# Four convolutions and a perceptron: outputs of two strips in one block

## The chip, the cores and the metric

The kernel runs on one core of a Trainium2 chip. A core has a matrix engine (TensorE, PE in the profile; its weight loads are PEld), a vector engine (VectorE, DVE), an activation engine (ScalarE, ACT), a general engine (GpSimd, POOL) and SyncE (SP), whose instruction queue issues most DMA transfers here. Each engine runs its own queue of instructions, and semaphores order them between engines. Matrix results go to PSUM, eight banks of 128 partitions x 512 float32; VectorE and ScalarE take them from there ("evict" them) to SBUF. The metric is the time of one execution on the device, in microseconds (us).

## The reference

The input is x of shape (4, 16, 512, 512), float32. Four layers follow each other, all with 16 channels in and out:

- layer 0: a depthwise 3x3 convolution with residual, attention in windows of 8x8, and a perceptron with 64 hidden units;
- layer 1: input and weights quantised to 8 bits, a 3x3 convolution, batch normalisation over the whole batch, a clip to 0..6;
- layer 2: two 3x3 convolutions with bias, a ReLU between them, and the input added;
- layer 3: a 3x3 convolution, and then at each pixel a perceptron with 128 hidden units, whose result is added to the layer's input.

Layer 3, which the change touches, is:

```python
y = conv3x3(x, conv_w)                                   # 16 -> 16 channels
h = relu(einsum('bchw,kc->bkhw', y, w1) + b1[None, :, None, None])   # 16 -> 128
upd = einsum('bkhw,ck->bchw', h, w2) + b2[None, :, None, None]       # 128 -> 16
return x + upd
```

## The kernel before

Layer 0 runs first and leaves its result in DRAM. `conv_layers` (L916) does the rest. A first pass over the data gives the statistics of layer 1's convolution; then a second pass, the tail, computes layers 1 to 3 for good. The change is in the tail alone.

**Layout.** The 512 image rows are cut into S = 4 strips of 128 rows, and each strip into M = 64 pairs of rows. One tile holds, for pair mm, all four images and all four strips: 128 partitions are four quarters of 32, and a quarter holds the two rows of the pair with 16 channels each. In the first layers a quarter is a strip and a free index is the image; the last convolution's results have it the other way round after a turn: a quarter is an image and a free index is a strip.

**One step.** The loop `for t in range(-2, M + 7)` (L1169) is a software pipeline. A step has four groups of matrix work, in this order:

1. the convolution of layer 3: it reads `x`, and `done3` (L1099) evicts its four banks to `y`, two by ScalarE and two by VectorE;
2. the second convolution of layer 2: it reads `h`, and `done2` (L1081) evicts to `x` with the residual added, all four by VectorE;
3. the first convolution of layer 2: it reads `z`, and `done1` (L1064) evicts to `h`, two by each engine;
4. the convolution of layer 1 in bfloat16: it reads `q`, and `done0` (L1052) evicts to `z`, all four by ScalarE.

Each convolution works on a different pair, so that a group needs only what earlier groups or steps have left. After group 2, `turned` (L1090) issues 16 DMA copies on SP that bring x into the layout by images (`xi`), for the residual of layer 3.

**A convolution** is 24 turns (`_conv_turn`, L905, matrix instruction in L908). A turn is four matmuls of 32x32 weights on one quarter i of the rows, for the four column quarters, and writes bank i of `conv_banks`. The turns go round the four quarters.

**The perceptron** is cut into units of work. `hidden` (L1112) makes one image's 128 hidden units for one row of one strip: four matmuls of 32x32 weights (L1117) on the quarter of that image into one bank of `hid_banks`, and an eviction with bias and ReLU to a tile `hid`, by ScalarE (L1123) for five of eight, by VectorE (L1125) for three. Eight of them are one strip of one pair. `output` (L1128) makes the results of that strip: eight matmuls with 128 rows and 32 columns (L1131) into `out_bank`, in which the two rows of an image are accumulated, an addition of bias and residual by VectorE (L1137) into `o`, and with the fourth strip the store to DRAM from SP.

**Order.** TensorE, VectorE, ScalarE and SP run in the order in which the program is written (`manual_schedule`); no planner changes it. `group` (L1143) writes the order within a group. It has 32 slots. Slots 4, 7, 10, ... 25 issue one `hidden` each, of the strip that the group was given, and one small piece of other work from the list `between` (a clip of z on VectorE; a scaling on VectorE or a rounding on ScalarE of the next q). The other 24 slots are the convolution's turns. Then come the convolution's evictions, and then `output` for the strip of the group before. So there are four output blocks in a step, one after each group, between the matmuls of one convolution and those of the next.

**Banks.** Of the eight, four are the convolution's, three (`hid_banks`, used in turn) the hidden units', one the outputs'.

Of the kernel before, what the change touches and what calls it, by code (L numbers as in the profile page):

```python
# [11 lines left out]
F32 = mybir.dt.float32  # L12
BF16 = mybir.dt.bfloat16
AF = mybir.ActivationFunctionType
ALU = mybir.AluOpType
# [8 lines left out]
B, C, H, W = 4, 16, 512, 512  # L24
P = 128
# [3 lines left out]
S = 4  # L29
M = H // S // 2  # L30
# [83 lines left out]
def conv_chain(ctx: ExitStack, tc: tile.TileContext, x, xw, mats, vecs, cqs, cws, hots, out):  # L114
# [32 lines left out]
    with tc.If(safe == 0):  # L147
        attention_block(tc, x, x1, m, v, peak)
    conv_layers(tc, x1, out, cw, cq, sw, m, v, peak)


# [728 lines left out]
def _quad(i):  # L880
    return slice(32 * i, 32 * i + 32)
# [18 lines left out]
def _turns():  # L900

    return [(side, dx, i) for side in range(2) for dx in range(3) for i in range(4)]


def _conv_turn(nc, p, weights, src, side, dx, i):  # L905

    for j in range(4):
        nc.tensor.matmul(  # L908
            p[i][_quad(j)], weights[_quad(i), side, dx, :],
            src[side][_quad(i), j, dx : dx + W],  # L910
            start=side == 0 and dx == 0, stop=side == 1 and dx == 2,
        )
# [3 lines left out]
def conv_layers(ctx: ExitStack, tc, x1, out, cw, cq, sw, m, v, peak):  # L916
# [18 lines left out]
    nc = tc.nc  # L935
    ld = ctx.enter_context(tc.tile_pool(name="l3l", bufs=2))
# [1 line left out]
    ps = ctx.enter_context(tc.tile_pool(name="l3p", bufs=1, space=PSUM))  # L938

    banks = [ps.tile([P, W], F32, name=f"tb{i}") for i in range(8)]  # L940
    conv_banks, hid_banks, out_bank = banks[0:4], banks[4:7], banks[7]

    def ring(name, n, dt=F32):
        tiles = []
        for i in range(n):
            t = act.tile([P, 4, WP], dt, name=f"{name}{i}")
            nc.gpsimd.memset(t[:, :, 0 : WP : WP - 1], 0.0)
            tiles.append(t)
        return lambda mm: tiles[mm % n]

    qs = ring("q", 3, BF16)
    zs, hs, xs, xi, ys = ring("z", 3), ring("h", 2), ring("x", 2), ring("xi", 3), ring("y", 2)

    edge_b1 = act.tile([P, 2], F32, name="edge_b1")
    nc.vector.tensor_scalar(edge_b1, v("edge"), v("l2_b1"), None, ALU.mult)
# [13 lines left out]
    def inner(t):  # L969
        return t[:, :, 1 : W + 1]  # L970
# [7 lines left out]
    def load(mm, tag="x"):  # L978
        loaded[mm] = ld.tile([P, S, W], F32, tag=tag, name=f"tx{mm}")
        _load_pairs(nc, loaded[mm], x1, mm)  # L980

    def scaled(mm, at=slice(0, S)):
        t = loaded[mm][:, at]
        nc.vector.tensor_scalar(t, t, ix, ROUND, ALU.mult, ALU.add)

    def rounded(mm, at=slice(0, S)):
        nc.scalar.activation(  # L987
            inner(qs(mm))[:, at], loaded[mm][:, at], AF.Identity, bias=unround
        )
# [9 lines left out]
    for mm in range(M):  # L999
# [5 lines left out]
        p = banks[4 * (mm % 2) : 4 * (mm % 2) + 4]  # L1005
# [19 lines left out]
    def mul(a, b, name):  # L1025
        t = act.tile([P, 1], F32, name=f"mul_{name}")
        nc.vector.tensor_tensor(t, a, b, ALU.mult)
        return t
# [9 lines left out]
    s = mul(sx, sw, "s")  # L1038
# [19 lines left out]
    def clipped(mm, b):  # L1058
        z = inner(zs(mm))
        nc.vector.tensor_scalar(z[:, b], z[:, b], ACT_MAX, None, ALU.min)  # L1060
        if outside(mm) is not None:
            nc.vector.memset(z[_quad(outside(mm)), b], 0.0)  # L1062
# [27 lines left out]
    def turned(mm):  # L1090

        if outside(mm) is None:
            for b in range(B):
                for s in range(S):
                    nc.sync.dma_start(
                        inner(xi(mm))[_quad(b), s, :], inner(xs(mm))[_quad(s), b, :]
                    )
# [10 lines left out]
    w2 = m("w2").rearrange("p (w n) -> p w n", w=2)  # L1108
    count = iter(range(1 << 30))
    waiting, outs = [], {}  # L1110

    def hidden(mm, s, par, b):  # L1112

        k = next(count)
        p = hid_banks[k % 3]
        for c in range(4):
            nc.tensor.matmul(  # L1117
                p[_quad(c)], w1[_quad(b), 1 - par, 32 * c : 32 * c + 32],
                inner(ys(mm + par))[_quad(b), s, :], start=True, stop=True,
            )  # L1120
        hd = ld.tile([P, W], F32, tag="hid", name=f"hid{mm}_{s}_{par}_{b}", bufs=16)
        if k % 8 in (0, 2, 3, 5, 6):
            nc.scalar.activation(hd, p, AF.Relu, bias=v("l3_b1"))  # L1123
        else:
            nc.vector.tensor_scalar(hd, p, v("l3_b1"), 0.0, ALU.add, ALU.max)  # L1125
        return b, par, hd

    def output():  # L1128
        mm, s, hids = waiting.pop(0)
        for b, par, hd in hids:  # L1130
            nc.tensor.matmul(  # L1131
                out_bank[_quad(b), :], w2[:, par], hd, start=par == 0, stop=par == 1
            )
        if s == 0:
            outs["o"] = ld.tile([P, S, W], F32, tag="o", name=f"o{mm}")
        o = outs["o"]
        nc.vector.scalar_tensor_tensor(  # L1137
            o[:, s, :], out_bank, v("l3_b2"), inner(xi(mm))[:, s, :], ALU.add, ALU.add
        )
        if s == S - 1:  # L1140
            nc.sync.dma_start(out[mm], o)

    def group(conv, unit, between):  # L1143


        turns, hids = iter(_turns() if conv else []), []
        for i in range(32):
            q, rest = divmod(i - 4, 3)
            if i >= 4 and rest == 0 and q < 8:
                if unit:  # L1150
                    hids.append(hidden(*unit, q // 4, i % 4))
                if between:
                    between.pop(0)()
            elif conv:
                _conv_turn(nc, conv_banks, conv[0], conv[1], *next(turns))
        for f in between:
            f()
        if conv:
            conv[2]()
        if waiting:  # L1160
            output()
        if unit:
            waiting.append((*unit, hids))

    def conv(layer, rows, lo, done, mm):
        weights = cq if layer is None else cw[:, layer]
        return weights, (rows(lo), rows(lo + 1)), lambda: done(mm)

    for t in range(-2, M + 7):  # L1169
        if t + 3 <= M + 2:  # L1170
            load(t + 3)
        new = [lambda s=s: scaled(t + 2, slice(s, s + 1)) for s in range(S)]
        new += [lambda s=s: rounded(t + 2, slice(s, s + 1)) for s in range(S)]
        clip = [lambda b=b: clipped(t - 1, b) for b in range(B)]
        mm = t - 4
        group(
            conv(2, xs, mm - 1, done3, mm) if 0 <= mm <= M else None,
            (t - 6, 3) if 0 <= t - 6 < M else None,
            clip if -2 <= t - 1 <= M + 1 else [],
        )  # L1180
        mm = t - 3
        group(
            conv(1, hs, mm, done2, mm) if -1 <= mm <= M else None,
            (t - 5, 0) if 0 <= t - 5 < M else None,
            new if t + 2 <= M + 2 else [],
        )
        if -1 <= mm <= M:
            turned(mm)
        mm = t - 1
        group(  # L1190
            conv(0, zs, mm - 1, done1, mm) if -1 <= mm <= M + 1 else None,
            (t - 5, 1) if 0 <= t - 5 < M else None, [],
        )
        mm = t
        group(
            conv(None, qs, mm, done0, mm) if -2 <= mm <= M + 1 else None,
            (t - 5, 2) if 0 <= t - 5 < M else None, [],
        )
    while waiting:
        output()  # L1200


def _strips(a):
# [128 lines left out]
```

## Time and profile before

| what | value |
|---|---|
| median of three runs | 6609.31 us (6609.27 to 6616.03) |
| the profiled execution | 6619.37 us |
| its span | 6617.5 us |
| TensorE busy, share of the span | 6388.5 us, 97% |
| ScalarE busy | 4209.4 us, 64% |
| VectorE busy | 3192.7 us, 48% |
| float32 convolution turns (L908, on z, x and h) | mean 597 to 603 ns a record |
| hidden units, TensorE (L1117) | 16384 records, mean 597 ns |
| hidden units, ScalarE and VectorE | 1280 of 687 ns, 768 of 751 ns |
| outputs, TensorE (L1131) | 4096 records, mean 605 ns |
| outputs, VectorE (L1137) | 256 of 751 ns (median) |

How to read it. The span is the time from the first instruction to the last. A row of the groups gives the line, the engine, the operation, the tile written and the tile read, the shape, the number of records, and after the bar the busy time, the mean of one in ns, and the idle time before it with what ended it. A float32 matmul has two records, one for each of two passes; a bfloat16 one has one. Records on different 32x32 parts of the array overlap, so a busy TensorE is not one at its peak. In the chain of work and in the timeline the first number is the start in us from the start of the span, the second the length of the merged piece, and the number after x is that of the records merged. Brackets give the idle time of the engine just before and what ended it.

### The profile page before, as it was taken

The numbers are of one execution on the slowest core, as the hardware profiler recorded it, in microseconds if no ns is written. First come the engines' busy times: TensorE is split into PE (matmuls) and PEld (weight loads), VectorE is DVE, ScalarE is ACT, GpSimd is POOL, SyncE is SP. The second block draws the span as 40 slices with busy tenths as digits, with TensorE's granted clock in tenths as the row PEclk, the third lists the DMA queues.
The fourth block names the chain that finished last, engine by engine and source line by source line (L and its number), as shares of the span: only waits on it lengthen the run. The fifth ranks groups of instructions, "written<-read, shape, count | busy, mean of one in ns | idle before, by whom it ended". The sixth has DMA issues, their size and how long they took to land. (4 is left out here: it accounts for less than half of the span.)

```text
span 6617.5 us, 317160 instructions
## 1 busy us (share of the span) xinstructions
PE 6388.5 (97%) x146976; PEld 3295.4 (50%) x146976; DVE 3192.7 (48%) x4640; ACT 4209.4 (64%) x5738; POOL 5.9 (0%) x25
## 2 busy tenths in 40 slices
PE   8999999999999999999996689999999999999998
PEld 5555555555555555555553344444444444444443
DVE  3444444444444444444445944444444444444444
ACT  5777777777777777777774545554555555555553
POOL 0000000000000000000000000000000000000000
PEclk9999999999999999999997789999999999999999
DMA  3333232333333333333324722222222222222221
GB/s 81 65 67 76 57 75 59 73 60 72 60 72 60 72 61 70 62 70 62 70 44 165 275 85 79 79 79 76 76 78 78 78 78 75 75 79 79 79 63 47
DMA packets 544391, 515.30 MB, mean 78 GB/s; under 512 B 349008, under 2 KB 480208, under 8 KB 514384
## 3 DMA queue, kind: packets, MB, share of 16 engines
q1 hardware_dynamic: 542768, 494.52, 28.6%
q8 instruction: 1154, 18.91, 1.2%
q14 instruction: 181, 1.48, 0.1%
q10 hardware_dynamic: 288, 0.39, 0.0%
HBM read 225.87 MB, written 134.48 MB: 54 GB/s over the span
## 5 line engine op out<-in xcount | busy, mean ns | idle before, releaser
L1117 PE MATMUL tb<-y,mat 32*32 32x512 f32 x16384 | 1684.6, 597 | 14.0 <-ACT hid L1123 7.5
L1123 ACT ACTIVATE hid<-tb,vec 128x512 f32<-128x512 f32 x1280 | 877.0, 687 | 1231.0 <-PE tb L1117 1205.6
L1125 DVE TENSOR_SCALAR hid<-tb,vec 128x512 f32<-128x512 f32 x768 | 576.8, 751 | 1173.9 <-PE tb L1117 860.5
L367 ACT ACTIVATE e<-pair 128x1024 f32<-128x1024 f32 x1024 | 992.4, 1021 | 225.7 <-PE pair L359 225.0
L295 PE MATMUL pair<-x,taps 32*32 32x512 f32 x18432 | 968.1, 606 | 1.9 <-ACT y L306 1.3
L416 PE MATMUL bank<-y,fc_e 32*32 32x512 f32 x8192 | 878.4, 607 | 3.7 <-ACT hid L421 3.1
L421 ACT ACTIVATE hid<-bank,f1b 128x512 f32<-128x512 f32 x1024 | 679.3, 686 | 298.3 <-PE bank L416 284.6
L351 DVE COPY yt<-bank 128x512 f32<-128x512 f32 x512 | 353.7, 691 | 905.8 <-PE bank L346 905.5
L1117 PEld LDWEIGHTS tb<-y,mat 32*32 32x32 f32 x16384 | 500.3, 103 | 406.0 <-issue 242.8
L359 PE MATMUL pair<-g,y 32*128 32x128 f32 x16384 | 652.2, 285 | 39.7 <-ACT e L367 38.7
L908 PE MATMUL tb<-z,cw 32*32 32x512 f32 x12864 | 643.8, 603 | 4.0 <-ACT z L1054 3.4
L359 PEld LDWEIGHTS pair<-g,y 32*128 32x128 f32 x16384 | 541.4, 186 | 185.9 <-ACT e L367 108.8
L908 PE MATMUL tb<-x,cw 32*32 32x512 f32 x12480 | 632.0, 597 | 1.5 <-ACT z L1054 1.5
L908 PE MATMUL tb<-h,cw 32*32 32x512 f32 x12672 | 628.6, 601 | 1.8 <-ACT z L1054 1.5
L295 PEld LDWEIGHTS pair<-x,taps 32*32 32x32 f32 x18432 | 459.0, 103 | 288.8 <-issue 183.7
L908 PE MATMUL tb<-q,cq 32*32 32x512 bf16 x12672 | 446.5, 436 | 122.1 <-ACT q L987 97.9
L378 PE MATMUL bank<-e,yt 128*32 128x128 f32 x16384 | 555.3, 276 | 0.9 <-ACT r L393 0.9
L383 PE MATMUL bank<-e,hot 128*32 128x512 f32 x4096 | 534.4, 592 | 0.0
L1131 PE MATMUL tb<-hid,mat 128*32 128x512 f32 x4096 | 498.5, 605 | 0.9 <-DVE o L1137 0.9
L378 PEld LDWEIGHTS bank<-e,yt 128*32 128x32 f32 x16384 | 417.7, 109 | 108.1 <-DVE yt L351 52.8
L429 DVE TENSOR_TENSOR xo<-bank,y 128x512 f32<-128x512 f32 x256 | 177.1, 692 | 546.2 <-PE bank L427 544.4
L346 PEld LDWEIGHTS bank<-mat,y 128*128 128x128 f32 x2048 | 215.2, 141 | 430.2 <-issue 376.5
(150 smaller groups left out, 6608.8 us busy)
## 6 DMA issues: line engine op xcount, KB each, us to landing
tx<-x SPq DMA_DIRECT2D x128, 1024.0 KB, 5.2
x<-in_xw_dram SPq DMA_DIRECT2D x32, 2600.0 KB, 9.9
y<-y SPq DMA_DIRECT2D x2048, 32.0 KB, 2.2
xi<-x SPq DMA_DIRECT2D x1024, 64.0 KB, 2.8
out_dram<-o SPq DMA_DIRECT2D x64, 1024.0 KB, 4.1
x<-xo SPq DMA_DIRECT2D x2000, 32.0 KB, 1.7
tx<-x SPq DMA_DIRECT2D x4, 768.0 KB, 4.2
x<-xo SPq DMA_DIRECT2D x48, 24.0 KB, 1.6
```

The source lines that it names most:

```text
L295: nc.tensor.matmul(bank(u)[quad(vv)], taps[quad(u), tap, :], xts[n // 2][quad(u), vv, dy : dy + WS, at : at + BW], start=tap == 0, stop=ta ...
L359: nc.tensor.matmul(bank(u)[:, P * jj : P * jj + P], y2[quad(u), vv, jl + jj].rearrange("p w t -> p (w t)"), g[quad(u), vv, jl + jj].rearra ...
L367: nc.scalar.activation(e[:, 2 * i : 2 * i + 2].rearrange("p u j t -> p u (j t)"), pairs[i], AF.Exp,)
L378: nc.tensor.matmul(b[quad(u), P * jj : P * jj + P], yt[:, jj, quad(u)], e[:, u, jj, :], start=True, stop=True,)
L383: nc.tensor.matmul(d[quad(u)], own, e[:, u].rearrange("p j t -> p (j t)"), start=True, stop=True,)
L416: nc.tensor.matmul(b[quad(k)], fc1[quad(vv), quad(k)], y[quad(vv), u, :], start=True, stop=True,)
L421: nc.scalar.activation(hd, b, AF.Gelu, bias=f1b)
L908: nc.tensor.matmul(p[i][_quad(j)], weights[_quad(i), side, dx, :], src[side][_quad(i), j, dx : dx + W], start=side == 0 and dx == 0, stop= ...
L1117: nc.tensor.matmul(p[_quad(c)], w1[_quad(b), 1 - par, 32 * c : 32 * c + 32], inner(ys(mm + par))[_quad(b), s, :], start=True, stop=True,)
L1123: nc.scalar.activation(hd, p, AF.Relu, bias=v("l3_b1"))
L1125: nc.vector.tensor_scalar(hd, p, v("l3_b1"), 0.0, ALU.add, ALU.max)
L1131: nc.tensor.matmul(out_bank[_quad(b), :], w2[:, par], hd, start=par == 0, stop=par == 1)
```

## The change

The outputs of two strips are made in one block. `outputs` takes the place of `output`: it runs only when two strips wait, which is after groups 2 and 4, and its two strips are those of the group just written and of the group before. It has no bank of its own: it uses the first two of `hid_banks`, of which there are now four. The hidden units of groups 2 and 4 stand in other slots (EARLY: four at the head of the group, and four more between slots 9 and 18), those of groups 1 and 3 where they were (LATE). The strips move by one group: strip 0 belongs to group 3, 1 to group 4, and 2 and 3 to groups 1 and 2 of the next step. `y` has three tiles in place of two. The number of instructions of each kind is the same.

```diff
-    conv_banks, hid_banks, out_bank = banks[0:4], banks[4:7], banks[7]
+    conv_banks, hid_banks = banks[0:4], banks[4:8]
...
-    zs, hs, xs, xi, ys = ring("z", 3), ring("h", 2), ring("x", 2), ring("xi", 3), ring("y", 2)
+    zs, hs, xs, xi, ys = ring("z", 3), ring("h", 2), ring("x", 2), ring("xi", 3), ring("y", 3)
...
-        p = hid_banks[k % 3]
+        p = hid_banks[k % 4]
...
-    def output():
-        mm, s, hids = waiting.pop(0)
-        for b, par, hd in hids:
-            nc.tensor.matmul(
-                out_bank[_quad(b), :], w2[:, par], hd, start=par == 0, stop=par == 1
-            )
-        if s == 0:
-            outs["o"] = ld.tile([P, S, W], F32, tag="o", name=f"o{mm}")
-        o = outs["o"]
-        nc.vector.scalar_tensor_tensor(
-            o[:, s, :], out_bank, v("l3_b2"), inner(xi(mm))[:, s, :], ALU.add, ALU.add
-        )
-        if s == S - 1:
-            nc.sync.dma_start(out[mm], o)
-
-    def group(conv, unit, between):
+    def outputs():
+        for p in hid_banks[0:2]:
+            mm, s, hids = waiting.pop(0)
+            for b, par, hd in hids:
+                nc.tensor.matmul(
+                    p[_quad(b), :], w2[:, par], hd, start=par == 0, stop=par == 1
+                )
+            if s == 0:
+                outs["o"] = ld.tile([P, S, W], F32, tag="o", name=f"o{mm}")
+            o = outs["o"]
+            nc.vector.scalar_tensor_tensor(
+                o[:, s, :], p, v("l3_b2"), inner(xi(mm))[:, s, :], ALU.add, ALU.add
+            )
+            if s == S - 1:
+                nc.sync.dma_start(out[mm], o)
+
+    def group(conv, unit, between, at):
         turns, hids = iter(_turns() if conv else []), []
         for i in range(32):
-            q, rest = divmod(i - 4, 3)
-            if i >= 4 and rest == 0 and q < 8:
+            if i in at:
                 if unit:
-                    hids.append(hidden(*unit, q // 4, i % 4))
+                    hids.append(hidden(*unit, len(hids) // 4, i % 4))
                 if between:
                     between.pop(0)()
             elif conv:
...
         if conv:
             conv[2]()
-        if waiting:
-            output()
         if unit:
             waiting.append((*unit, hids))
+        if len(waiting) == 2:
+            outputs()
+
+    LATE, EARLY = range(4, 28, 3), (0, 1, 2, 3, 9, 12, 15, 18)
...
         group(
             conv(2, xs, mm - 1, done3, mm) if 0 <= mm <= M else None,
-            (t - 6, 3) if 0 <= t - 6 < M else None,
-            clip if -2 <= t - 1 <= M + 1 else [],
+            (t - 6, 2) if 0 <= t - 6 < M else None,
+            clip if -2 <= t - 1 <= M + 1 else [], LATE,
         )
...
         group(
             conv(1, hs, mm, done2, mm) if -1 <= mm <= M else None,
-            (t - 5, 0) if 0 <= t - 5 < M else None,
-            new if t + 2 <= M + 2 else [],
+            (t - 6, 3) if 0 <= t - 6 < M else None,
+            new if t + 2 <= M + 2 else [], EARLY,
         )
...
         group(
             conv(0, zs, mm - 1, done1, mm) if -1 <= mm <= M + 1 else None,
-            (t - 5, 1) if 0 <= t - 5 < M else None, [],
+            (t - 5, 0) if 0 <= t - 5 < M else None, [], LATE,
         )
...
         group(
             conv(None, qs, mm, done0, mm) if -2 <= mm <= M + 1 else None,
-            (t - 5, 2) if 0 <= t - 5 < M else None, [],
-        )
-    while waiting:
-        output()
+            (t - 5, 1) if 0 <= t - 5 < M else None, [], EARLY,
+        )
```

## The prediction

> **What bounds the kernel now.** I read the page first, then the chain that ended last inside one step of the tail, then the timeline at each kind of boundary.
>
> ```profile
> span 6617.5 us, 317160 instructions
> ...
> PE 6388.5 (97%) x146976; PEld 3295.4 (50%) x146976; DVE 3192.7 (48%) x4640; ACT 4209.4 (64%) x5738; POOL 5.9 (0%) x25
> ...
> L1131 PE MATMUL tb<-hid,mat 128*32 128x512 f32 x4096 | 498.5, 605 | 0.9 <-DVE o L1137 0.9
> ```
>
> TensorE is bound; ScalarE and VectorE have room on average. What counts is how TensorE's time splits inside a step. I call the four groups of a step A (conv on x, writes y), B (on h, writes x), C (on z, writes h) and D (bfloat16, on q, writes z). The chain gives the output blocks (start, length) that close B, C, D, A and B again:
>
> ```profile
> 4990.94 1.85 PE tb L1131 x16
> ...
> 5002.32 1.85 PE tb L1131 x16
> ...
> 5009.81 1.85 PE tb L1131 x16
> ...
> 5021.38 1.85 PE tb L1131 x16
> ...
> 5032.76 1.85 PE tb L1131 x16
> ```
>
> So C takes 11.38 us, D 7.49, A 11.57, B 11.38, with their blocks: a step is 41.82 us. There are 60 full steps. The PE timeline of one B and the start of the next C:
>
> ```profile
> 5026.21 0.66 PE L1117 MATMUL tb<-y,mat 32*32 32x512 f32 x4
> ...
> 5028.44 0.66 PE L1117 MATMUL tb<-y,mat 32*32 32x512 f32 x4
> ...
> 5029.43 0.66 PE L1117 MATMUL tb<-y,mat 32*32 32x512 f32 x4
> ...
> 5030.47 0.60 PE L1117 MATMUL tb<-y,mat 32*32 32x512 f32 x2
> ...
> 5032.69 1.92 PE L1131 MATMUL tb<-hid,mat 128*32 128x512 f32 x16
> 5034.54 1.11 PE L908 MATMUL tb<-z,cw 32*32 32x512 f32 x28
> ```
>
> A turn is four matmuls on one quarter of the rows, each in two passes; four turns on four different quarters run at once, a round. Rounds follow each other every 1.06: from 5026.21 to 5030.47 are four. Single starts of the same timeline: B's last pass begins 9.01 after its first, 0.52 later the block begins, its four waves start 0.43 apart (1.33), and 0.52 after the last the next conv begins. The block thus takes 0.52 + 1.33 + 0.52 = 2.37 between convs (2.16 after D, 0.30 + 1.33 + 0.52), of which four waves are 1.72[...].
>
> Step: 9.20 (A) + 2.37 + 9.01 (B) + 2.37 + 9.01 (C) + 2.37 + 5.33 (D) + 2.16 = 41.82. A's extra 0.19 and D's length are explained here:
>
> ```profile
> 5006.23 0.13 PEld L1117 LDWEIGHTS tb<-y,mat 32*32 32x32 f32 x5 [0.50 <-ACT hid L1123]
> ...
> 5006.59 0.15 PEld L1117 LDWEIGHTS tb<-y,mat 32*32 32x32 f32 x8 [0.21 <-DVE hid L1125]
> ...
> 5008.16 0.13 PEld L1117 LDWEIGHTS tb<-y,mat 32*32 32x32 f32 x5 [0.27 <-ACT hid L1123]
> ...
> 5009.94 2.78 ACT L1054 ACTIVATE z<-tb,shift,scale 128x512 f32<-128x512 f32 x4
> ...
> 5012.77 0.13 PEld L908 LDWEIGHTS tb<-x,cw 32*32 32x32 f32 x5 [0.52 <-ACT z L1054]
> ```
>
> In D a first-layer unit waits for one of three banks, twice in a row: from a unit's first pass to its eviction 1.17, eviction 0.69 to 0.75, so 1.93 a bank. At A's start the fourth conv bank comes 1.1 late, ScalarE emptying all four; it costs only the 0.19, the next round hiding the rest.
>
> [...] VectorE does x's four evictions before the output's add. [...] after a turn that is blocked on its own quarter only two later turns start. I use this: a turn starts when its quarter is free and the fourth turn before it is done.
>
> **The change, part by part.**
>
> 1. Blocks. Before: 3 x 2.37 + 2.16 = 9.27 a step. After: two blocks of eight waves, 0.52 + 1.33 + 4 x 0.429 + 0.52 = 4.09 after B, 3.87 after D: 7.96. Gain 1.31.
>
> 2. A's stall. The block before A now lasts 3.87 from D's last pass; z's four evictions ended 3.28 after it. The 0.19 goes. After B, x's evictions (2.71 on VectorE, from about its last pass) are covered by 4.09.
>
> 3. B's order. LATE, by the rule: 0123, then quarter 0 twice running, and so on: nine rounds where eight would do, as the trace has them. EARLY: units on 0,1,2,3, convs on 0,1,2,3, then 0 1 1 2 0 3 0 3 1 2 2 3 and three times 0123: again nine, the last with two quarters. No gain there. But B now follows A without a block, so its first round comes 1.06, not 0.88, after the last: nine rounds of 1.06, 9.54 from A's last pass to B's last, where B had 9.01. Loss 0.53.
>
> 4. Covers at that boundary. How evictions run by two engines is shown after C:
>
> ```profile
> 5001.37 0.69 ACT L1079 ACTIVATE h<-tb,vec 128x512 f32<-128x512 f32 x1 [0.50 <-PE tb L908]
> ...
> 5002.20 1.41 DVE L1077 TENSOR_SCALAR h<-tb,vec 128x512 f32<-128x512 f32 x2 [0.31 <-PE tb L908]
> ...
> 5002.29 0.69 ACT L1079 ACTIVATE h<-tb,vec 128x512 f32<-128x512 f32 x1 [0.23 <-PE tb L908]
> ```
>
> From C's last pass (5001.74) the banks are free at 0.33, 1.22, 1.24, 1.87. Before, 2.37 of block hid this. Now one round of units does: they pass at about 0.4 to 0.6, the convs could follow at 1.5 to 1.6. Only the fourth bank is late, by 0.3, and its quarter idles in the next half-filled round: cost nothing; without that slack 0.3 a boundary. Behind a waiting conv stand all later turns on TensorE; ScalarE and VectorE go on.
>  The new wait: the fifth unit (turn 9) needs the first unit's bank. Its data are ready 1.17 after its first pass, at 1.2 to 1.75, ScalarE is free from 1.24, so it is evicted by 1.93 to 2.45; turn 9 wants to start at 2.6. On time, by 0.15 at worst. In B, VectorE has one scaling (0.48) before the second unit's eviction and three behind it: bank 1 free at 3.0, wanted at 3.8. The four roundings stand seven slots earlier in ScalarE's queue than before, behind the third and fourth unit's evictions (over by 3.8); no bank is wanted before that. Cost nothing.
>
> 5. D. From C's last pass: four units at -0.4 to 0.6; convs at 1.2 to 1.9; fifth unit 2.0 to 2.5; sixth when bank 1 is free, 2.65; seventh [...] 3.0 to 3.5; eighth when the sixth is done or bank 3 free (three evictions in a row on ScalarE: 1.5 + 3 x 0.69), 3.65 to 3.9; its quarter is free 0.95 later, and three conv turns of 0.25 follow on it: last start 5.2 to 5.6. I take 5.40, where D had 5.33 after its block. Loss 0.07. The units thus lose one of two waits for a bank, but four of them now run first, while C is still being evicted.
>
> 6. Moved work. Outputs of strips 0 and 2 come one group later, those of 1 and 3 where they were. The adds (0.75 each) of the pair stand behind x's or z's evictions; the first ends about 4 after B's last pass, the second 4.9, and the next units want these banks at about 5.0 and 5.8. The store of a row block stays ahead of the 16 turning copies on SP, both some 2 us later; those copies are read two steps later. The third y tile only lets A's evictions run while B reads older rows. Nothing on the path.
>
> Sum: -1.31 - 0.19 + 0.53 + 0.07 = -0.90; step 40.92. Times 60: -54. At the end of the tail there are eight groups with units alone in place of seven, but each about 1 shorter with four banks (5.04 before) and four pair blocks for seven; one conv group has lost its units: together -3, between -10 and +3. The profiled execution took 6619.4 (span 6617.5 and 1.9 around it); 6562 comes out. The median of the runs shown is 10 below the profiled one: 6552.
>
> **The rivals.** *Fewer rounds:* if TensorE looks further ahead than my rule, EARLY fits in eight rounds: another 1.06 in B, step 39.86, 118 + 3 saved: 6488. Against it: LATE would then also take eight. *D keeps its length:* if the fifth to eighth units still come one after another behind ScalarE, D takes 6.0 instead of 5.4: step 41.52, 6588; with 0.3 in B as well, no change (6606). For it: ScalarE has five of eight units. *Evictions at the head, slower:* in B and D the convs and the fifth unit wait for conv evictions and unit evictions queued on the same two engines with one round as cover. If turn 9 starts at 3.4 (all four units' evictions after the last conv eviction, one behind the other) B costs 0.76 more and D 1.0: step 42.68, 6658. It decides from 0.90 a step, 0.45 in each of B and D. Against it: the times in 4, which leave 0.15.
>
> **How the numbers follow.** Forecast 0.61 (own range 6525 to 6585), D's length 0.20, slower 0.11, fewer rounds 0.08. Below 6510 lies most of the last, above 6604 the slower case and a piece of the second: some 0.2. Faster by over 0.2% (13 us, about what this measurement tells): 0.60 + 0.14 + 0.08 = 0.82; within: 0.06; slower 0.12.
>
> **What will show it.** Right: blocks of 32 records, two a step, step 40.9; B's nine rounds following A at 1.06; no wait for z at A's start; D's last pass 5.4 after C's. Wrong: weight loads in B or D waiting for unit or conv evictions over 0.5 a group; a round count other than nine; a wave spacing in the long block over 0.43 (second unit's hidden tiles late).

## The result and the profile after

The changed kernel took 6497.38 us (median of four, 6489.81 to 6500.31), the kernel before 6611.19 (four runs). The ratio is 0.982, with a 95% interval of 0.981 to 0.983: faster by some 114 us, where 57 were forecast, and below the range. The profiled execution of the changed kernel has a span of 6497.8 us, 119.7 less than before.

The page of the changed kernel, with the lines that answer to those of before; the outputs are L1133 now:

```profile
span 6497.8 us, 317055 instructions
...
PE 6264.0 (96%) x146976; PEld 3402.1 (52%) x146976; DVE 3186.5 (49%) x4640; ACT 4179.7 (64%) x5738; POOL 6.0 (0%) x26
...
L1133 PE MATMUL tb<-hid,mat 128*32 128x512 f32 x4096 | 471.1, 601 | 0.0
```

The numbers of matrix, VectorE and ScalarE instructions are the same, VectorE and ScalarE do what they did; TensorE's busy time fell by 124.5, about what the span fell (119.7). Its chain through one step (start, length; the blocks after B, after D, and after B again):

```profile
4500.56 3.57 PE tb L1133 x32
...
4518.49 3.57 PE tb L1133 x32
...
4540.66 3.57 PE tb L1133 x32
```

There are two blocks of 32 records, each 3.57 long where one of 16 was 1.85. From 4500.56 to 4540.66 a step is 40.10 us, where it was 41.82. The table shows how it is made up, from the starts of single records, which the views merge. A pass is one of the two records of a float32 matmul; a wave is four records of a block side by side. Where no block lies between two groups, a group is counted from the last pass of the one before.

| piece of a step | before | forecast | after |
|---|---|---|---|
| A, first pass to last | 9.20 | 9.01 | 9.00 |
| block after A | 2.37 | none | none |
| B (before: first to last; else from A's last to B's last) | 9.01 | 9.54 | 9.08 |
| block after B, conv to conv | 2.37 | 4.09 | 4.09 |
| C | 9.01 | 9.01 | 9.01 |
| block after C | 2.37 | none | none |
| D (before: first to last; else from C's last to D's last) | 5.33 | 5.40 | 5.05 |
| block after D | 2.16 | 3.87 | 3.87 |
| step | 41.82 | 40.92 | 40.10 |

Blocks, A and C came as forecast to 0.02. B came 0.46 and D 0.35 below the forecast; that is all of the 0.82 by which the step was missed. Sixty steps make 103 of the 119.7 us. Before, steps of the tail also had a mean 0.14 above their median (41.954 and 41.814 over fifty of them), after the two agree (40.104 and 40.10): about 8 us over sixty steps. The remaining 9 or so lie at the two ends.

Two views of B and D show what was taken wrongly. First the PE timeline in B: the first passes of the sixth, seventh and eighth unit.

```profile
4533.96 0.62 PE L1117 MATMUL tb<-y,mat 32*32 32x512 f32 x2
...
4535.28 0.66 PE L1117 MATMUL tb<-y,mat 32*32 32x512 f32 x4
...
4536.33 0.60 PE L1117 MATMUL tb<-y,mat 32*32 32x512 f32 x2
```

The head's last unit starts at 4531.62 (single starts). Sixth, seventh and eighth follow 2.3, 3.7 and 4.7 us later, where three, four and five rounds of 1.06 make 3.2, 4.2 and 5.3. From the eighth to the last pass at 4540.07 it is 3.74, as forecast (three rounds and a second pass, 3.6 to 3.8). The time was thus saved in the first three rounds: they took 2.3 where I had 3.2, and the fourth gave 0.3 back (1.3 for 1.06). By my rule the third and the fourth held three turns each, the others four, but the last two. The rule is an estimate of mine from the timeline of the kernel before: in its B, whose first pass is at 5023.16, the first and the second unit (turns 5 and 8) start 0.88 and 1.26 later, the third (turn 11) 3.04 later, two rounds on, as the rule has it. What in TensorE makes it so was not shown. Then the evictions and weight loads at the change from C to D:

```profile
4512.70 0.69 ACT L1079 ACTIVATE h<-tb,vec 128x512 f32<-128x512 f32 x1 [0.50 <-PE tb L908]
...
4513.53 1.41 DVE L1077 TENSOR_SCALAR h<-tb,vec 128x512 f32<-128x512 f32 x2 [0.25 <-PE tb L908]
4513.62 0.69 ACT L1079 ACTIVATE h<-tb,vec 128x512 f32<-128x512 f32 x1 [0.23 <-PE tb L908]
...
4514.21 1.84 ACT L1123 ACTIVATE hid<-tb,vec 128x512 f32<-128x512 f32 x3
...
4514.33 0.13 PEld L908 LDWEIGHTS <-cq 32*32 32x32 bf16 x8 [0.48 <-issue]
4514.85 0.74 DVE L1125 TENSOR_SCALAR hid<-tb,vec 128x512 f32<-128x512 f32 x1
4514.99 0.11 PEld L908 LDWEIGHTS <-cq 32*32 32x32 bf16 x7 [0.53 <-issue]
...
4515.65 0.13 PEld L1117 LDWEIGHTS tb<-y,mat 32*32 32x32 f32 x5
```

The three units of D's head that ScalarE evicts follow each other without a gap, 1.84 for the three, 0.57 apart where single ones last 0.69. The eighth unit did not wait for its bank: the fourth unit's was free at 4516.05, 2.99 after C's last pass (4513.06), and the eighth began at 3.67. But other work of D waited. "Issue" means that the profile shows no releaser; the convolution turns loaded at 4514.99 start 0.05 after VectorE had emptied the last bank of h (4513.53 + 1.41), 1.93 after C's last pass, and the chain of work runs through this eviction. The sixth unit, too, is loaded (4515.65) 0.05 after VectorE had given back the second unit's bank; so it is in each of 44 steps.

### The profile page after: what moved, and what is told of

Same layout as the page of the kernel before. It is cut to its first block, busy times and chain, and to the rows that moved or that the text cites. A ratio compares the mean times of both kernels' runs of the same rounds, so it can differ in the third digit from the quotient of the medians.

```text
span 6497.8 us, 317055 instructions
## 1 busy us (share of the span) xinstructions
PE 6264.0 (96%) x146976; PEld 3402.1 (52%) x146976; DVE 3186.5 (49%) x4640; ACT 4179.7 (64%) x5738; POOL 6.0 (0%) x26
## 5 line engine op out<-in xcount | busy, mean ns | idle before, releaser
L1123 ACT ACTIVATE hid<-tb,vec 128x512 f32<-128x512 f32 x1280 | 847.5, 687 | 1127.8 <-PE tb L1117 1126.5
L1117 PE MATMUL tb<-y,mat 32*32 32x512 f32 x16384 | 1567.9, 599 | 2.0 <-DVE o L1139 1.3
L1125 DVE TENSOR_SCALAR hid<-tb,vec 128x512 f32<-128x512 f32 x768 | 575.3, 749 | 890.0 <-PE tb L1117 872.8
L908 PE MATMUL tb<-h,cw 32*32 32x512 f32 x12672 | 590.7, 601 | 1.8 <-ACT z L1054 1.5
L908 PE MATMUL tb<-q,cq 32*32 32x512 bf16 x12672 | 418.5, 424 | 138.4 <-ACT q L987 103.2
L1133 PE MATMUL tb<-hid,mat 128*32 128x512 f32 x4096 | 471.1, 601 | 0.0
```

The lines of the kernel that those rows point to most:

```text
L908: nc.tensor.matmul(p[i][_quad(j)], weights[_quad(i), side, dx, :], src[side][_quad(i), j, dx : dx + W], start=side == 0 and dx == 0, stop= ...
L1117: nc.tensor.matmul(p[_quad(c)], w1[_quad(b), 1 - par, 32 * c : 32 * c + 32], inner(ys(mm + par))[_quad(b), s, :], start=True, stop=True,)
L1133: nc.tensor.matmul(p[_quad(b), :], w2[:, par], hd, start=par == 0, stop=par == 1)
```

## The experiments

Each starts from the changed kernel or from the kernel before, as its heading or first line says; ratios are to runs of the kernel before on the same chip. "Step" is the median over fifty steps of the tail.

### Three banks

```diff
-        p = hid_banks[k % 4]
+        p = hid_banks[k % 3]
...
-        for p in hid_banks[0:2]:
+        for p in (hid_banks[3], hid_banks[(turn[0] + 2) % 3]):
```

(`turn[0]` is the number of units issued so far: the second output takes the unit bank that is needed last.)

> The changed kernel with three banks for the hidden units in place of four (the outputs take the free one and the unit bank needed last). If the fourth bank carries D's gain: the fourth unit at the head of B and D waits for the first one's eviction, D goes from 5.05 us (last pass of C to last pass of D) to 5.9 or more and B from 9.08 to about 9.5, the step from 40.10 to 41.3, the time to about 6570. If the slots carry it and the bank little: step within 0.2 of 40.10, time within 12 of 6497.

Measured: ratio 1.0026 (1.0014 to 1.0038), 6639 us. B is 9.77, D 6.24, the step 41.98: 1.88 more than with four, and the whole gain is gone. What TensorE's weight loads waited for, over the tail (total us, times, longest; units are L1119 and L1125 in this kernel, outputs L1135):

```profile
PEld tb L1119 <- ACT hid L1125: 104.6, 90, 1.2
...
PEld tb L908 <- ACT z L1054: 37.7, 45, 0.8
```

The 90 waits of 1.2 are two a step, one at the head of B and one at the head of D: the fourth unit waits there for the first one's eviction, and all convolution turns stand behind it. The direction is the one expected, the size half as large again. The second row is the 0.84 after a block in which its last wave runs while no weights are loaded; the kernel before and the changed one have it too.

### LATE slots in all groups

```diff
-    LATE, EARLY = range(4, 28, 3), (0, 1, 2, 3, 9, 12, 15, 18)
+    LATE = EARLY = range(4, 28, 3)
```

> The changed kernel with the LATE slots in all four groups. If the units at the head are the cover for the conv evictions: B and D begin with conv turns that wait for their banks, up to 1.8 us after the last pass of the group before; B goes from 9.08 to about 9.8 and D from 5.05 to about 6.3, the step to 42.0, the time to about 6610. If only pair blocks and the fourth bank matter: step within 0.3 of 40.10, time 6497 to 6515.

Measured: ratio 1.0012 (1.0002 to 1.0022), 6629 us; B 9.82, D 6.51, the step 42.30. As the first theory had it, to 0.3. The waits:

```profile
PEld tb L908 <- DVE y L1103: 53.9, 90, 0.8
```

Ninety times, twice a step over forty-five steps, a convolution turn at B's head waits for an eviction of y by VectorE; in the changed kernel such waits are 48 and 17.1 us over the same window, one a step. D's head waits for h, as the chain shows (DVE h, 1.42 long): the turn that needs the last bank starts 1.93 after C's last pass in both kernels, but in the changed one four units have run by then beside three turns, here the three turns alone. So merging the blocks, even with the fourth bank, is worth nothing by itself: it takes the cover from two of four boundaries.

### Four banks for the kernel before

```diff
-    conv_banks, hid_banks, out_bank = banks[0:4], banks[4:7], banks[7]
+    conv_banks, hid_banks, out_bank = banks[0:4], banks[4:8], banks[7]
...
-        p = hid_banks[k % 3]
+        p = hid_banks[k % 4]
```

> The kernel before with four banks for the units, the fourth lent to the output blocks, all else as it was. If three banks held D back by themselves: D's 5.33 us become about 4.5, the step 41.0, the time about 6560. If the slots are what matters in D (each unit is followed there by a conv turn on its own quarter): D stays above 5.1, the time above 6597.

Measured: ratio 1.0004 (0.9994 to 1.0014). D fell from 5.33 to 4.77, but the block after it came 1.10 later, not 0.30: the lent bank was the eighth unit's, whose eviction is the last. The step stayed at 41.87. So the run was repeated with another bank lent (`out_bank = banks[4]`):

> The kernel before with four banks for the units, and the bank that is needed last before the block (the one of the units at slots 4 and 16) lent to it; the run with the fourth bank lent had D's last pass 4.77 us after its first in place of 5.33, but its block waited 0.8 more for the lent bank. If that wait was only the choice of bank: D stays at 4.8, its block follows 0.30 later, the step is 41.2 to 41.3, the time about 6580. If four banks give the kernel before nothing: step 41.8 again.

Measured: ratio 1.0014 (1.0005 to 1.0023); the block now follows after 0.30, but D is 5.51 long and the step 42.00. The waits tell why:

```profile
PEld tb L1117 <- DVE o L1137: 81.1, 121, 0.8
```

The first unit now waits for the output's addition to give its bank back. In D it comes 0.23 after the group's start, its bfloat16 turns being short (one record of 0.38 a matmul, where float32 has two of 0.59), and the addition ends at 0.89. With either of the two banks that were lent, a block after every group costs the kernel before what the fourth bank brings: the expected 6580 was wrong. In the changed kernel there is no block ahead of B and D, the groups that begin with units, and A and C come to their first unit only at 0.88.

### One strip a block, all else as changed

```diff
-        for p in hid_banks[0:2]:
+        for p in hid_banks[3:4]:
...
-        if len(waiting) == 2:
+        if waiting:
```

> The changed kernel with an output block of one strip after every group, of the group just written, in a lent bank; slots and banks as changed. If filling and emptying TensorE at each block is the price: two more of them add 1.3 us a step, and the first round of B and D after one is 0.2 shorter each and finds its banks free, so the step goes to 41.0 to 41.3, the time to 6550 to 6570. If merging the blocks gave nothing: step within 0.2 of 40.10.

Measured: ratio 0.995 (0.993 to 0.9969), 6590 us; the step is 41.49, 1.39 more than with pairs. It was 0.2 to 0.5 above what was expected. By single starts the blocks take 9.58 a step in place of 7.96: 1.31 for two more of them, as expected (that the price is one of filling and emptying TensorE is not shown by it), and 0.31 because the block after D starts 0.61 after D's last pass, not 0.30: it makes the strip just written and waits for the eviction of its last units. B and D are shorter by 0.10 and 0.13, where 0.2 each was expected. There the fourth unit at the head waits for the lent bank:

```profile
PEld tb L1117 <- DVE o L1139: 68.0, 92, 0.7
```

These are two waits a step of 0.74 each. They can account for the missing 0.1 in B and in D, but little more: the first convolution turn starts 0.98 after the first unit, where a first round after a block takes 0.88. So in the changed kernel the merged blocks are worth 1.39 a step: 1.62 in the blocks, less 0.23 in B and D.

### Full rounds in A, B and C

```diff
-    LATE, EARLY = range(4, 28, 3), (0, 1, 2, 3, 9, 12, 15, 18)
+    LATE, EARLY = (4, 5, 6, 7, 20, 21, 22, 23), (0, 1, 2, 3, 16, 17, 18, 19)
+    MIXED = (0, 1, 2, 3, 9, 12, 15, 18)
```

(MIXED, the old EARLY, stays in D.)

> The changed kernel with units in bursts of four in A, B and C (A and C: slots 4 to 7 and 20 to 23; B: 0 to 3 and 16 to 19; D as changed), so that turns go round the four quarters without a break: eight full rounds a group in place of nine that are partly filled. If a full round costs 1.06 whatever its neighbours: A and C end their last pass 7.95 us after their first (9.00 before), B 8.5 after A's (9.08), the step is 37.4, the time about 6335. If the 1.06 comes from turns that wait for their own quarter, full rounds go at 0.88: A and C about 6.9, B 7.1, step 34, time about 6130. If the number of rounds isn't what sets a group's length: step within 0.3 of 40.10.

Measured: ratio 0.961 (0.957 to 0.965), 6355 us; the step is 37.73. A and C take 8.18 (9.00 before), B 8.41 (9.08), D 5.00. Blocks on the chain, after D, B, and D:

```profile
4630.15 3.57 PE tb L1133 x32
...
4650.82 3.57 PE tb L1133 x32
...
4668.09 3.57 PE tb L1133 x32
```

From D's block to B's it is 20.67, where the changed kernel has 22.17 (4518.49 to 4540.66). Eight full rounds in B in 8.41 are 1.05 each, as a full round was priced; A and C took 0.23 more than expected. Nine rounds, some in part filled, are only 0.67 more in B, 0.82 in A: that is what one round more costs when it comes from such gaps, not 1.06.

### Full rounds in D too

```diff
-    MIXED = (0, 1, 2, 3, 9, 12, 15, 18)
```

(and D takes EARLY as just changed)

> As the run with full rounds in A, B and C, and D too has its units at slots 0 to 3 and 16 to 19. If D is bound by ScalarE's evictions of its units (0.57 to 0.69 each, five of eight): the second burst waits for its banks and D stays at 5.0 to 5.4 us. If it is bound by conv turns that wait for a quarter held by a unit: D falls to about 4.4, 0.6 a step, 36 us less than the run before.

Measured: ratio 0.956 (0.953 to 0.959), 6318 us; D 4.37, the step 37.10, 0.63 less. So ScalarE's evictions did not set D's 5.00. That convolution turns waiting for a quarter did, as the expectation has it, is not shown: with the units at slots 16 to 19 the sixth unit's wait for the bank that VectorE empties goes too. This version beats both kernels; by the two ratios (0.956 and 0.982) it is 2.7% under the changed one.

### Full rounds in the kernel before

With four banks, `out_bank = banks[4]`, and

```diff
-            q, rest = divmod(i - 4, 3)
-            if i >= 4 and rest == 0 and q < 8:
+            if i in (4, 5, 6, 7, 20, 21, 22, 23):
...
-                    hids.append(hidden(*unit, q // 4, i % 4))
+                    hids.append(hidden(*unit, len(hids) // 4, i % 4))
```

> As the run before, four blocks of one strip, and the units in bursts at slots 4 to 7 and 20 to 23 in all four groups. If the number of rounds sets a group's length whatever the blocks: A, B and C end 0.8 us sooner each (8.2 in place of 9.0), D goes to about 4.2, the step to 38.0, the time to about 6385. If the gain of full rounds needs the merged blocks and the units at the head: step above 40.5.

Measured: ratio 0.975 (0.972 to 0.978), 6448 us; A, B and C 8.18 to 8.20, D 5.17, the step 38.99. A, B and C as expected; D not: its first units wait for the output's addition as before, and the chain of work runs through it. Against the run with the same banks and the old slots (step 42.00) the order of quarters gives 3.01 a step, where the change itself gave 1.72, and it does not need the change.

### Ten rounds in B

```diff
+    SPREAD = (0, 1, 2, 3, 8, 13, 18, 23)
...
-            new if t + 2 <= M + 2 else [], EARLY,
+            new if t + 2 <= M + 2 else [], SPREAD,
```

> The changed kernel with B's last four units at slots 8, 13, 18 and 23 in place of 9, 12, 15 and 18: each is then followed by a conv turn on its own quarter, and by the rule of the prediction (a turn starts when its quarter is free and the fourth turn before it is done) B takes ten rounds, most of them with three turns. If the rule holds and a part-filled round costs 0.7 to 1.06: B's last pass 9.7 to 10.1 after A's (9.08 with nine rounds), the step 40.7 to 41.1, the time 6535 to 6560. If only the work of each quarter counts: B stays within 0.2 of 9.08.

Measured: ratio 0.986 (0.983 to 0.989), 6519 us; B 9.44, the step 40.46. Of the four moved units only the first is followed at once by a turn on its own quarter (after the others one, two and three turns on other quarters come first); by the rule the order makes ten rounds all the same. B grew by 0.36: more than "only the work of each quarter" allows, less than ten rounds at 0.7 or above. The rule orders the three slot lists rightly (eight rounds 8.41, nine 9.08, ten 9.44), but its rounds have no fixed price.

## Why the prediction was wrong

The direction and the chain of reasons held; two terms of the sum were mis-sized, both as losses that did not come.

- *Part 1, blocks, gain 1.31, and part 2, A's stall, 0.19:* both as forecast, to 0.02. The second strip's hidden tiles were never late; the eight waves stayed 0.43 apart.
- *Part 3, B at nine rounds of 1.06, 9.54, a loss of 0.53:* this step failed. B took 9.08, a loss of 0.07. I priced every round as a full one. Eight full rounds do cost 1.05 each; but by the rule the third and the fourth round hold three turns and the last one two, and a round more costs 0.67 in B when it comes from such gaps. Why was not tested. In the trace the first passes of B's last round start closer together (0.09 from first to last, 0.24 in a full round). And the first three rounds took 2.3 for 3.2, while by the rule only the third is part-filled. Turns of the second were late there, since they waited for evictions of y (the weight loads stood idle 0.36 for the first of them); that others ran faster meanwhile is likely, but not shown.
- *Part 4, covers and the new wait, cost nothing:* right as to cost, and the runs show what stands behind it. A sign that I had named for being wrong did show in D: its convolution turns waited 0.48 and 0.53 for evictions of h. That lost nothing against the forecast, since part 5 has these turns at 1.2 to 1.9 after C's last pass, where the last came at 1.93. Without the units at the head B and D lose 2.20 a step together, without the fourth bank 1.88. Both figures are larger than the gain of the change, so that the whole gain stands on these covers. Neither the third tile of y nor the shift of the strips was tried alone; the table leaves no time for them.
- *Part 5, D at 5.40:* the second step that failed, by 0.35. Up to the eighth unit the working was right: it started 3.67 after C's last pass, within my 3.65 to 3.9, and the sixth came when its bank was free, at 2.59 (forecast 2.65). From there to the last start it was 1.38 where I had 1.55 to 1.7 (0.95 and three of 0.25 make 1.70): the last three turns of a quarter have two gaps between their starts, not three, of 0.2, not 0.25. I had also put ScalarE's evictions at 0.69 when they come 0.57 apart. Whether the sixth unit's bank or the quarters set D's length is open.
- *Part 6, moved work:* nothing on the path, as said. *The ends, 3:* the two ends gave about 9.
- *Left out:* the steps of the kernel before that are longer than the median. In twelve of fifty, each four steps or a multiple after the last, TensorE loses 0.2 to 0.6 at one and the same place of C, where the timeline has no releaser. One of them:

```profile
4286.56 0.13 PEld L1117 LDWEIGHTS tb<-y,mat 32*32 32x32 f32 x5 [1.14 <-issue]
```

  The weight loads stood idle for 1.14 with nothing that the profile shows to wait for. Such steps are gone in the changed kernel (some 8 us of its gain), but every run of the experiments has some, those that start from the changed kernel too (the mean 0.05 to 0.29 above the median; 37.90 and 37.73 with full rounds). These 8 us are thus not shown to come from the change. Their cause is open; transfers of instructions (queue q8) come back to the same places of C every four steps in both kernels (at 4284.3, 4452.0, 4620.0 before, at 4507.5, 4669.3, 4829.1 after), but whether they matter was not tested.

Of the rivals, *fewer rounds* gave the time that came closest, 6488, but by luck, not by its mechanism: B does not take eight rounds in the changed kernel, since eight take 8.41. *D keeps its length* was wrong, and *evictions at the head* is what the runs with three banks and with LATE slots look like.

## What to carry to other kernels

Where 32x32 tiles share TensorE, write the order so that consecutive turns go round the row quarters without a repeat: 3.0 us a step here (40.10 to 37.10, and 42.00 to 38.99), more than merging blocks and a fourth bank together (1.72), with the same instructions. Merging the blocks of another tiling in pairs saved 1.31 a step in blocks (9.27 to 7.96), but each block also covered the evictions at its boundary: put independent matrix work there, and enough banks for it, or the gain is gone (2.20 a step lost without the units at the head, 1.88 without the fourth bank). When pricing rounds from a profile, price a full and a part-filled one apart (here 1.05, and 0.67 to 0.82 for one more that comes from gaps).

## What the runs showed of the hardware

- In the changed kernel evictions that followed each other without a gap on ScalarE came 0.57 us apart (hidden units) and 0.66 (z; medians), where a single record is 0.69 and 0.78 long.
- Eight full rounds of sixteen 32x32 float32 tiles with 512 columns and two passes took 8.41 us in a running stream, 1.05 each (B of the run with full rounds in A, B and C); the first after a block of another tiling took 0.88 (B of the kernel before).
- A fourth bank for the units in the kernel before gave nothing (ratios 1.0004 and 1.0014) while one of the four, the first or the last, was lent to a block after every group.
